# Quarters for the fifth product of all pairs, ScalarE for each block's first slot, the bias kept in DRAM

## The chip, the core and the metric

The kernel runs on one NeuronCore of a Trainium2 chip. Its engines work side by side, each through its own instruction queue in order: TensorE (PE, matmuls; its weight loads are listed as PEld), VectorE (DVE), ScalarE (ACT), GpSimd (POOL) and SyncE (SP, which issues transfers). Transfers (DMA) are issued from the queues of SP, ACT and POOL and carried out by 16 DMA engines. SBUF is the on-chip memory of 128 partitions, PSUM the small memory that PE writes to, used here in banks of 128 x 512 fp32, DRAM the memory outside.

The metric is the device time of one execution in microseconds (us), the median of several runs. Lower is better.

## What is computed

One layer of a relational graph network with a highway gate, on 1250 nodes of 1024 features, 20000 edges of 8 types, all in fp32:

```python
h = jnp.maximum(_layernorm(x, axis=-1), 0.0)
# _rgcn(h, ...):
out = h @ root + bias
for r in range(8):
    mask = (edge_type == r).astype(x.dtype)
    sums = segment_sum(h[src] * mask[:, None], dst, num_segments=n)
    cnt = segment_sum(mask, dst, num_segments=n)
    out = out + (sums / jnp.maximum(cnt, 1.0)[:, None]) @ weight[r]
u = out
z = jnp.concatenate([u, h], axis=1) @ w_gate + b_gate
x = x + jnp.tanh(u) * z + h * (1.0 - z)
```

## The kernel before

**Matrices and steps.** The kernel multiplies first and gathers afterwards. It computes y_r = h @ weight[r] for all nodes and stores y in DRAM; for every edge it later fetches row src of y_r, scales it by one over the count, and adds it to u of node dst. With root and the two halves of w_gate there are 11 matrices of 1024 x 1024: s = 0 to 7 are the relations, 8 is root, 9 the half of w_gate that meets h, 10 the half that meets u. The nodes lie in ten blocks of 128 (the last has 98 rows), taken two at a time: step (s, i) with i = 0 to 4 multiplies blocks i and i + 5 by matrix s. So matrices 0 to 9 have 50 steps, some 115 us for the five of one matrix.

**Strassen.** Each step is a Strassen product of halves (Winograd's form): seven half products instead of eight, with operands A11, A12, S4, S1, S2, S3, A22 in `h_op[i]` and the matching weight combinations in `wbuf`. One half product is four calls of 128x512 (line 511), each of which is two matmuls in the trace. Where two steps form a pair, (0,1) or (2,3), some of their half products are themselves made by Strassen's scheme over the pair, by quarters (line 255, 128x256): `Second` for A12, `Third` for S4, `First` for A11, and `Fifth` for S1. A quarter scheme replaces two half products (16 matmuls of 512 in the trace) by seven quarter products (28 of 256). It also needs sums on DVE: `sums` and `next_sums` (lines 309 to 318, four operations each, through the shared buffers `room`), copies on ACT (lines 424, 432, 439) and two adds into PSUM (lines 434, 445). Step i = 4 stands alone.

**Which pairs make S1 by quarters.** `fifths(s, i)` decides: `FIFTHS = (1, 4)`, so both pairs for s = 1 to 4, and only pair (0,1) for s = 5 to 9. While it holds for a step, `narrow[0]` is set and `sum_bank(1)` keeps one of the four `ps` banks of PSUM for good (`kept`); the first time, `touch` writes to it with one bf16 matmul (line 134). At a step where `fifths` is false the kept bank is given up.

**A pair with Fifth.** In the pair's first step, `product` runs `root.begin()`, `p1` (with `First.late`, `root.sums()`, `root.second()`), the S2 product, `root.early()`, `root.next_sums()`, and within `p7`, after the S3 product, `between(TICK)` and `root.late()`. `late` begins with the quarter product that reads what L315 and L316 made.

**The order of work beside the products.** After each part of a product, `done()` calls `between(j)`, which runs whatever is due beside it: the sums for the next product, loads of weights, and the work of the edges. The program order written this way is the order in every engine's queue. From s = 5 on the work beside is `edges`, one generator that advances by a number of ticks at each call (`spread`): 

- Group 0 (relations 0 to 4) runs beside s = 5 to 7, group 1 (relations 5 to 7) beside s = 8 and 9.
- For each block of 128 nodes sorted by degree, `K[g][d]` slots: 118 in group 0, 75 in group 1. One slot is one tick, `add_slot`: an indirect gather of 128 rows of y on POOL's queue into one of five `got` buffers (line 1560), and u = got * w + u on DVE (line 1565).
- u starts from `first_u`: in group 0 by a load of the bias, repeated over the rows, on SP's queue (line 1578); in group 1 by a gather of what group 0 stored (line 897).
- Five ticks after the last slot, `u_back` stores u of group 0 into its rows of `u_dram` (line 903, an indirect store on POOL's queue).

Before that, beside s = 4, the generator `beside_group` waits for step (4, 2), makes `passes_over`, gives five calls away and then counts edges (`counts`, lines 934 and 935), the rest of which is worked off at the end of step (4, 3).

The two lines that give `spread` its pace:

```python
said[0] += (10, 8, 13, 11, 8)[at_call[0]]
while said[1] < min(total, -(-total * said[0] // parts)):
```

Of the kernel before, what the change touches and what calls it, by code (L numbers as in the profile page):

```python
# [15 lines left out]
OP = mybir.AluOpType  # L16
# [5 lines left out]
def tile_rgcn_highway(  # L22
# [472 lines left out]
    def product(aop, w, to, between=lambda j: None, last=None, pieces=1, whole=True,  # L495
# [67 lines left out]
        def p1():  # L563
            if first is None:
                b = lead()
                add(b, A11, True)
            else:
                b = first.late() if head else first.to1
            if root and head:
                root.sums()  # L570
                first.fifth_to()
            nc.scalar.copy(c11, b)  # L572
            if root and head:
                root.second()
            done()
            filled("first")
            return b

        def p5(c=None):
# [108 lines left out]

    def fifths(s, i=0):

        return s >= FIFTHS[0] and (s <= FIFTHS[1] or i < 2)

    waiting, waiting_third, waiting_first, waiting_fifth = {}, {}, {}, {}
    at_call = [0, 0]
# [203 lines left out]
            out=to, out_offset=None, in_=of,  # L898
            in_offset=bass.IndirectOffsetOnAxis(ap=at, axis=0), compute_op=op)

    def to_rows(of, frm, at, group):
        nc.gpsimd.memset(apart, 0.0)
        ins = nc.gpsimd.indirect_dma_start(  # L903
            out=of, out_offset=bass.IndirectOffsetOnAxis(ap=at, axis=0), in_=frm, in_offset=None)
        tc.declare_no_dep(ins.ins, query=no_wait, group=group, reason="rows differ")
        tc.add_to_no_dep_group(group, ins.ins)

# [620 lines left out]
    with ExitStack() as edges_part:  # L1528
# [25 lines left out]
            nc.vector.tensor_scalar_max(rcp, rcp, 1.0)  # L1554
            nc.vector.reciprocal(rcp, rcp)

        def add_slot(u, g, d, k, at, w):
            n = nrows(d)
            t = got()
            nc.gpsimd.indirect_dma_start(  # L1560
                out=t[:n], out_offset=None, in_=y[g][:, :],
                in_offset=bass.IndirectOffsetOnAxis(ap=at[:n, d, k:k + 1], axis=0),
                bounds_check=y[g].shape[0] - 1, oob_is_err=False)
            w = w[:n, d, k:k + 1]
            nc.vector.scalar_tensor_tensor(u[:n], t[:n], w, u[:n], op0=OP.mult, op1=OP.add)  # L1565

# [6 lines left out]
        def first_u(g, d):  # L1573

            n = nrows(d)
            u = new_u(d)
            if g == 0:
                nc.sync.dma_start(u[:n], bias[None, :].to_broadcast([n, D]))
            else:
                rows_of(u[:n], u_dram[g - 1][:, :], node[:n, g, d:d + 1])  # L1580
            return u

        def edges(g, blocks, to, late=0, more={}):

            nb = len(blocks)
            starts = [late + sum(K[g][d] for d in blocks[:b]) for b in range(nb + 1)]
            leaves = [starts[b + 1] - 1 + GOT for b in range(nb)]  # L1590
            reads = [max(-1, starts[b] - (9 if d in more else 5),
                         leaves[b - UB] if b >= UB else -1) for b, d in enumerate(blocks)]
            u, then = {}, {}
            for t in range(-1, leaves[-1] + 4):
                for b, d in enumerate(blocks):
                    if starts[b] <= t < starts[b + 1]:
                        k = t - starts[b]
                        add_slot(u[d], g, d, k, idx[:, g], w_of[:, g])
                for b, d in enumerate(blocks):
                    if t == leaves[b]:  # L1600
                        then[t + 3] = to(d, u[d])
                if then.get(t):
                    then[t]()
                for b, d in enumerate(blocks):
                    if t == reads[b]:
                        u[d] = first_u(g, d)
                    if d in more and t == starts[b] - 4:
                        more[d](d, u[d])
                yield

        def u_back(g):
            def to(d, u):
                n = nrows(d)
                to_rows(u_dram[g][:, :], u[:n], node[:n, g, d:d + 1], f"u{g}")

            return to

        def spread(e, total, parts):

            said = [0, 0]  # L1620
            parts *= 10

            def between(j):
                said[0] += (10, 8, 13, 11, 8)[at_call[0]]
                while said[1] < min(total, -(-total * said[0] // parts)):
                    next(e, None)
                    said[1] += 1
                if said[0] == parts:
                    for _ in e:
                        pass  # L1630

            return between
# [50 lines left out]
        def beside_group():  # L1683

            yield
            while at_call != [2, 1]:
                yield
            passes_over()
            for _ in range(5):
                yield  # L1690
            for g in range(G):
                yield from counts(g)
# [339 lines left out]
```

## Time and profile before

| what | us |
|---|---|
| median of 3 runs (lowest, highest) | 1329.66 (1327.8, 1329.93) |
| the profiled execution, its own time | 1325.06 |
| its span, first to last instruction | 1323.3 |
| busy in the span: PE, DVE, POOL, ACT | 1309.9, 1032.2, 642.6, 277.9 |
| slot adds on DVE (line 1565), 193 | 246.8, 1.282 each |
| gathers on POOL (line 1560), 193 | 255.4, 1.324 each |

Times in all views are microseconds from the span's start. A row of the timeline gives the start, the length from the first start to the last end, and how many equal instructions it merges; ends of matmuls are modelled and overlap the next start, so the distance between starts is the real cost. The steps that matter here lie at 543.3 to 585.0 (s = 4, i = 2 and 3), 612.5 to 657.5 and 657.5 to 699.9 (s = 5, pairs (0,1) and (2,3)), 957.7 (start of s = 8), 1003.0 to 1045.4 (s = 8, pair (2,3)) and 1118.1 to 1160.5 (s = 9, pair (2,3)).

### The profile page before, as it was taken

Reading aid. Unit: us, or ns where it says so; the run is one execution under the profiler, and the core shown is the slowest. Engines: PE = TensorE matmul, PEld = TensorE weight load, DVE = VectorE, ACT = ScalarE, POOL = GpSimd, SP = SyncE. Lnnn points to the kernel's source line nnn. Section 1 sums busy time; section 2 is a strip of 40 time slices with the busy share of each in tenths; the row PEclk is TensorE's granted clock in tenths of the full one; section 3 lists DMA queues with packets and bytes.
Section 4 is the critical chain, followed back from the end, with each engine's and each line's share of the span. In section 5 each row is a group of like instructions: output and inputs, shape, how many; then the busy total and the mean of one; then the engine's idle time right before and its main releaser. Section 6 shows DMA issues by size and latency. Waiting matters only on the chain.

```text
span 1323.3 us, 14353 instructions
## 1 busy us (share of the span) xinstructions
PE 1309.9 (99%) x4280; PEld 747.0 (56%) x4280; DVE 1032.2 (78%) x2171; ACT 277.9 (21%) x509; POOL 642.6 (49%) x981
## 2 busy tenths in 40 slices
PE   9999999999999999999999999999999999999997
PEld 5444565556455546655655655665565566544443
DVE  7768977797783776558977988897788889867974
ACT  3352121121112212211221211122122112122210
POOL 0001766666666675412453545456465546624732
PEclk9999999999999999999999999999999999999999
DMA  8976566753734253444748779788789957979961
GB/s 312 300 231 165 98 115 136 153 82 82 170 113 115 57 143 65 68 161 157 250 136 309 252 272 366 268 282 283 255 282 335 362 187 256 312 269 297 331 173 60
DMA packets 119397, 273.22 MB, mean 206 GB/s; under 512 B 33438, under 2 KB 45106, under 8 KB 119184
## 3 DMA queue, kind: packets, MB, share of 16 engines
q1 hardware_dynamic: 59120, 122.06, 31.7%
q0 software_dynamic: 44064, 118.20, 28.0%
q10 hardware_dynamic: 16128, 31.98, 7.9%
q8 instruction: 34, 0.56, 0.2%
q14 instruction: 51, 0.42, 0.1%
HBM read 210.73 MB, written 76.46 MB: 217 GB/s over the span
## 4 chain that ended last, share of the span: by engine, by line
PE 87%; DMA 4%; DVE 4%; issue 3%; POOL 1%; SPq 1%; ACT 1%; POOLq 0%; DVEq 0%
PE ps_b L511 42%; PE ps L255 19%; PE ps L511 10%; PE ps_n L511 4%; PE ps_b L255 4%; PE ps_n L255 3%; PE ps_q L255 2%; PE ps_q L511 2%; DMA xt<-in_x_dram 1%; DMA got<-hr_dram,node 1%; DMA w<-in_L_gnn_weight_dram 1%; DVE h_op L492 1%; DMA h_op<-in_L_gnn_b_gate_dram 0%; POOL out_dram L903 0%; SPq L983 0%
## 5 line engine op out<-in xcount | busy, mean ns | idle before, releaser
L511 PE MATMUL ps_b<-w,h_op 128*128 128x512 f32 x1464 | 658.3, 594 | 1.0 <-ACT row L615 0.8
L511 PEld LDWEIGHTS ps_b<-w,h_op 128*128 128x128 f32 x1464 | 275.2, 190 | 301.2 <-issue 292.7
L1560 POOL DMA_INDIRECT got<-y,idx x193 | 255.4, 1324 | 277.5 <-DVE u L1565 182.1
L1565 DVE SCALAR_TENSOR_TENSOR u<-got,w_of,u 128x1024 f32<-128x1024 f32 (+1 forms) x193 | 246.8, 1282 | 38.9 <-DMA got<-y,idx 36.3
L1209 POOL DMA_INDIRECT table<-row_col,at_i x157 | 183.3, 1168 | 119.4 <-issue 84.4
L511 PE MATMUL ps<-w,h_op 128*128 128x512 f32 (+1 forms) x392 | 174.1, 586 | 0.8 <-ACT row L589 0.8
L511 PEld LDWEIGHTS ps<-w,h_op 128*128 128x128 f32 x392 | 73.5, 190 | 84.0 <-issue 78.7
L255 PE MATMUL ps<-inner 128*128 128x256 f32 x420 | 106.1, 380 | 0.0
L255 PEld LDWEIGHTS ps<-inner 128*128 128x128 f32 x420 | 79.2, 190 | 20.7 <-issue 9.4
L255 PE MATMUL ps<-w,h_op 128*128 128x256 f32 x340 | 88.2, 382 | 1.0 <-ACT w L272 1.0
L255 PEld LDWEIGHTS ps<-w,h_op 128*128 128x128 f32 x340 | 63.7, 190 | 29.3 <-issue 20.7
L537 ACT COPY row<-ps_b 128x512 f32<-128x512 f32 x53 | 31.1, 586 | 225.4 <-PE ps_b L511 225.4
L615 ACT COPY row<-ps_b 128x512 f32<-128x512 f32 x54 | 31.7, 586 | 216.0 <-PE ps_b L511 216.0
L511 PE MATMUL ps_n<-w,h_op 128*128 128x512 f32 x168 | 75.6, 593 | 0.0
L255 PE MATMUL ps<-w,w 128*128 128x256 f32 x288 | 70.6, 380 | 0.0
L255 PEld LDWEIGHTS ps<-w,w 128*128 128x128 f32 x288 | 54.4, 190 | 17.2 <-issue 11.0
L1217 POOL MEMSET apart<- 128x1 f32 x471 | 54.6, 116 | 18.1
L659 ACT COPY row<-ps_b 128x512 f32<-128x512 f32 x40 | 23.4, 586 | 186.2 <-PE ps_b L511 165.1
L543 DVE TENSOR_TENSOR row<-row 128x512 f32<-128x512 f32 x44 | 30.2, 686 | 39.6 <-ACT row L537 39.6
L1326 DVE SCALAR_TENSOR_TENSOR junk<-k_bc,key_col,before 128x128 f32<-128x128 int16 x157 | 55.0, 350 | 4.2
L511 PEld LDWEIGHTS ps_n<-w,h_op 128*128 128x128 f32 x168 | 31.7, 190 | 37.7 <-issue 37.1
L572 ACT COPY row<-ps_b 128x512 f32<-128x512 f32 x54 | 31.8, 588 | 84.8 <-PE ps_b L511 80.5
(254 smaller groups left out, 1568.1 us busy)
## 6 DMA issues: line engine op xcount, KB each, us to landing
y<-row SPq DMA_DIRECT2D x72, 512.0 KB
w<-in_L_gnn_weight_dram ACTq DMA_DIRECT2D x21, 1024.0 KB
w<-in_L_gnn_weight_dram SPq DMA_DIRECT2D x10, 1024.0 KB
w<-lefts_dram SPq DMA_DIRECT2D x16, 512.0 KB
w<-in_L_gnn_w_gate_dram ACTq DMA_DIRECT2D x6, 1024.0 KB
k_bc<-keys_dram SPq DMA_DIRECT2D x39, 128.0 KB
l_bc<-los_dram SPq DMA_DIRECT2D x39, 128.0 KB
h_dram<-h_op SPq DMA_DIRECT2D x9, 512.0 KB
```

The costliest lines, as they stand in the source:

```text
L255: nc.tensor.matmul(p, a[:, k, :], b[:, k, :], start=(fresh and k == 0), stop=(k == 1), skip_group_check=True)
L511: nc.tensor.matmul(b[:, at], aop[:, i, k, :], w.of[i][:, k, at], start=(fresh and k == 0), stop=(k == KQ - 1), skip_group_check=True)
L537: nc.scalar.copy(d, b)
L543: nc.vector.tensor_add(c22, c if lone else c22, d)
L572: nc.scalar.copy(c11, b)
L615: nc.scalar.copy(c12, b)
L659: nc.scalar.copy(c21, b)
L1209: ins = nc.gpsimd.indirect_dma_start(out=table[:, :], out_offset=bass.IndirectOffsetOnAxis(ap=at_i[:n, c:c + 1], axis=0), in_=row_col[:n, ...
L1217: nc.gpsimd.memset(apart, 0.0)
L1326: nc.vector.scalar_tensor_tensor(junk, o["k_bc"][:, i, :], key_col[:, c:c + 1], before, op0=OP.is_equal, op1=OP.mult, accum_out=rank[:, c: ...
L1560: nc.gpsimd.indirect_dma_start(out=t[:n], out_offset=None, in_=y[g][:, :], in_offset=bass.IndirectOffsetOnAxis(ap=at[:n, d, k:k + 1], axis=0),
L1565: nc.vector.scalar_tensor_tensor(u[:n], t[:n], w, u[:n], op0=OP.mult, op1=OP.add)
```

## The change

- `fifths` becomes true for all s > 0: pair (2,3) of s = 5 to 9 makes S1 by quarters too, and the kept bank stays from s = 1 on.
- `spread` no longer counts the additional call `TICK`, except at i = 0, so that i = 2 keeps its pace.
- In the second step of a pair (`root and inner and not head`) the fills that belong to p1 run ahead of `done()` instead of after it.
- In group 0 each block's first slot makes u on ScalarE: the gather is issued two ticks ahead of the copy (`slot_of`), the copy scales it into a new u (`scaled_slot`). Group 0's ticks fall from 123 to 113.
- The bias no longer starts u. Instead `beside_group` writes it into all rows of `u_dram`, from DRAM to DRAM on SP's queue, in ten calls where it gave five away, and `u_back` stores with an add.

```diff
@@ product, p1
-            done()
-            filled("first")
+            if root and inner and not head:
+                filled("first")
+                done()
+            else:
+                done()
+                filled("first")
             return b
@@
     def fifths(s, i=0):
-        return s >= FIFTHS[0] and (s <= FIFTHS[1] or i < 2)
+        return s > 0
@@
-    def to_rows(of, frm, at, group):
+    def to_rows(of, frm, at, group, op=OP.bypass):
         nc.gpsimd.memset(apart, 0.0)
         ins = nc.gpsimd.indirect_dma_start(
-            out=of, out_offset=bass.IndirectOffsetOnAxis(ap=at, axis=0), in_=frm, in_offset=None)
+            out=of, out_offset=bass.IndirectOffsetOnAxis(ap=at, axis=0), in_=frm, in_offset=None,
+            compute_op=op)
@@
-            if g == 0:
-                nc.sync.dma_start(u[:n], bias[None, :].to_broadcast([n, D]))
-            else:
-                rows_of(u[:n], u_dram[g - 1][:, :], node[:n, g, d:d + 1])
+            rows_of(u[:n], u_dram[g - 1][:, :], node[:n, g, d:d + 1])
             return u
+        def scaled_slot(t, g, d):
+            n = nrows(d)
+            u = new_u(d)
+            nc.scalar.mul(u[:n], t[:n], w_of[:n, g, d, 0:1])
+            return u
@@ edges
-            starts = [late + sum(K[g][d] for d in blocks[:b]) for b in range(nb + 1)]
+            by_act = int(g == 0)
+            starts = [late + sum(K[g][d] - by_act for d in blocks[:b]) for b in range(nb + 1)]
...
-                        k = t - starts[b]
+                        k = t - starts[b] + by_act
                         add_slot(u[d], g, d, k, idx[:, g], w_of[:, g])
...
-                    if t == reads[b]:
+                    if by_act:
+                        if t == starts[b] - 3:
+                            ahead[d] = slot_of(g, d, 0, idx[:, g])
+                        if t == starts[b] - 1:
+                            u[d] = scaled_slot(ahead.pop(d), g, d)
+                    elif t == reads[b]:
                         u[d] = first_u(g, d)
@@ u_back
-                to_rows(u_dram[g][:, :], u[:n], node[:n, g, d:d + 1], f"u{g}")
+                to_rows(u_dram[g][:, :], u[:n], node[:n, g, d:d + 1], f"u{g}", OP.add)
@@ spread
-                said[0] += (10, 8, 13, 11, 8)[at_call[0]]
+                if j != TICK or at_call[0] == 0:
+                    said[0] += (10, 8, 13, 11, 8)[at_call[0]]
@@ beside_group
-            for _ in range(5):
+            for d in range(ND):
+                nc.sync.dma_start(u_dram[0][block(d), :],
+                                  bias[None, :].to_broadcast([nrows(d), D]))
                 yield
@@
-        s, i = beside(first_group, sum(K[0]) + LATE + 1, s, i, R0[2] - 1)
+        s, i = beside(first_group, sum(K[0]) - ND + LATE + 1, s, i, R0[2] - 1)
```

`slot_of` is the gather of `add_slot`, taken out into a function of its own; `add_slot` now calls it.

More of the change, by code (lines that the diff above doesn't have):

```diff
@@ L1555, in as_reciprocals, with slot_of @@
             nc.vector.reciprocal(rcp, rcp)
-        def add_slot(u, g, d, k, at, w):
+        def slot_of(g, d, k, at):
             n = nrows(d)
@@ L1563, in add_slot @@
                 bounds_check=y[g].shape[0] - 1, oob_is_err=False)
+            return t
+        def add_slot(u, g, d, k, at, w):
+            n = nrows(d)
+            t = slot_of(g, d, k, at)
             w = w[:n, d, k:k + 1]
@@ L1576, in first_u @@
             u = new_u(d)
-            if g == 0:
-                nc.sync.dma_start(u[:n], bias[None, :].to_broadcast([n, D]))
-            else:
-                rows_of(u[:n], u_dram[g - 1][:, :], node[:n, g, d:d + 1])
+            rows_of(u[:n], u_dram[g - 1][:, :], node[:n, g, d:d + 1])
+            return u
+        def scaled_slot(t, g, d):
+            n = nrows(d)
+            u = new_u(d)
+            nc.scalar.mul(u[:n], t[:n], w_of[:n, g, d, 0:1])
             return u
@@ L1592, in edges @@
                          leaves[b - UB] if b >= UB else -1) for b, d in enumerate(blocks)]
-            u, then = {}, {}
+            u, then, ahead = {}, {}, {}
             for t in range(-1, leaves[-1] + 4):
```

## The prediction

> **What bounds the kernel now.** I read the page first: engine rows, clock slices, chain.
>
> ```profile
> span 1323.3 us, 14353 instructions
> PE 1309.9 (99%) x4280; PEld 747.0 (56%) x4280; DVE 1032.2 (78%) x2171; ACT 277.9 (21%) x509; POOL 642.6 (49%) x981
> PEclk9999999999999999999999999999999999999999
> PE 87%; DMA 4%; DVE 4%; issue 3%; POOL 1%; SPq 1%; ACT 1%; POOLq 0%; DVEq 0%
> ```
>
> TensorE (PE) has work for 99% of the span at the full granted clock, and is 87% of the chain that ended last. A busy PE is not yet a PE without waits, so next I read the timeline of PE by start times: the distance from one start to the next is what a group really costs.
>
> ```profile
> 654.01 3.60 PE L511 MATMUL ps_b<-w,h_op 128*128 128x512 f32 x8
> 657.45 3.60 PE L511 MATMUL ps_n<-w,h_op 128*128 128x512 f32 x8
> 660.88 1.03 PE L255 MATMUL ps<-inner 128*128 128x256 f32 x4
> 661.75 1.03 PE L255 MATMUL ps_b<-w,inner 128*128 128x256 f32 x4
> ...
> 682.60 3.60 PE L511 MATMUL ps<-w,h_op 128*128 128x512 f32 x8
> 686.04 3.60 PE L511 MATMUL ps_b<-w,h_op 128*128 128x512 f32 x8
> ...
> 741.36 0.38 PE L134 MATMUL ps<-ident 128*128 128x512 bf16 x1
> 741.58 1.03 PE L255 MATMUL ps<-inner 128*128 128x256 f32 x4
> ```
>
> Eight 512-wide matmuls take 3.43 us from start to start (657.45 to 660.88), 0.429 each; four 256-wide ones 0.86, 0.2155 each. Neighbouring groups start at these distances throughout matrices 4 to 9; nothing waits there beyond 0.1 us now and then. So in this stretch the time is the count of matmuls, and any PE work removed is time removed, unless a wait appears. Whether one can appear is read from VectorE (DVE), by stages.
>
> ```profile
> 543.30:585.00 41.70, 41.70 (x147) 27.13 (x146) 23.03 (x57) 9.77 (x20) 14.13 (x15) 1.00 0.35 101
> 657.45:699.87 42.42, 42.42 (x133) 24.83 (x132) 34.55 (x42) 8.57 (x17) 24.14 (x20) 1.00 0.52 168
> 1003.00:1045.40 42.40, 42.40 (x133) 24.82 (x132) 32.04 (x38) 8.57 (x17) 27.48 (x22) 1.00 0.97 343
> 1118.10:1160.50 42.40, 42.40 (x133) 24.83 (x132) 34.61 (x44) 8.57 (x17) 27.65 (x21) 1.00 0.94 317
> 612.50:657.50 45.00, 45.00 (x162) 30.18 (x161) 44.16 (x89) 9.82 (x21) 19.54 (x15) 1.00 0.76 249
> ```
>
> Columns: stretch, length, busy PE, weight loads, DVE, ACT, POOL, clock, DMA share, GB/s. Rows one to four are steps i=2 and 3 of matrices 4, 5, 8 and 9; the last is i=0 and 1 of matrix 5. Matrix 4 already makes this pair's S1 product by quarters, matrix 5 does not: that comparison is the heart of the forecast.
>
> **The change, part by part.** (1) *Quarters.* With `fifths` true for all s > 0, pair (2,3) of matrices 5 to 9, five pairs, replaces two S1 products (16 matmuls of 512 in the trace, 16 x 0.429 = 6.87 us) by seven quarter products (28 of 256, 28 x 0.2155 = 6.03): -0.83 us. The rows confirm it: 42.42 at matrix 5 against 41.70 at matrix 4, where one stray transpose (L1657, 551.17 to 551.28, 0.11) is included: 42.42 - 41.59 = 0.83. Five pairs: -4.15 us.
>
> [...]
>
> (2) *The kept bank.* It is now never given up between matrices 5 and 9, so four `touch` matmuls (i=0 of matrices 6 to 9) go: 741.36 to 741.58, 0.22 each, -0.88 us. The price: three rotating banks instead of four in i=2 to 4. Matrices 1 to 4 run that way, and the bank row that was closest at matrix 4 (L283, ended 569.91, reused 574.59) left 4.7 us. Zero.
>
> Sum of what is removed from PE: -5.03 us.
>
> (3) *What quarters add elsewhere.* Per pair DVE gets four 128x256 operations (0.417), four 128x512 (0.683) and two into PSUM (0.425): 5.25 us. ACT gets 0.36 + 0.37 + 0.57, in handshakes with PE that are already in the 41.59. DVE in the pair goes from 34.55 to 39.8 of 41.6 us at matrix 5, from 32.04 to 37.3 at matrix 8, from 34.61 to 39.9 (96%) at matrix 9, before the relief of (4). It still fits; the last row shows 98% busy without a PE wait. What counts is one deadline: the sums L315 and L316 must end before PE's `late`. Their margin under load, at i=0 of matrix 5:
>
> ```profile
> 622.41 2.28 DVE L207 TENSOR_TENSOR w<-w,w 128x2048 f32<-128x2048 f32 x1
> 624.61 0.42 DVE L434 TENSOR_TENSOR ps_n<-ps,inner 128x256 f32<-128x256 f32 x1
> 625.27 0.68 DVE L316 TENSOR_TENSOR inner<-w 128x512 f32<-128x512 f32 x1
> 626.37 1.03 PE L255 MATMUL ps<-inner 128*128 128x256 f32 x4
> ```
>
> L316 ends at 625.95, PE starts at 626.37: 0.42 us left, the tightest of the five; with an idle DVE (matrix 4, i=2) it was 556.44 - 554.63 = 1.8. At i=2 two slot adds (1.28 each, 1.2 apart) stand just before L434. From the end of `First.late` PE needs 0.86 + 3.43 + 1.72 = 6.0 us to L434's input (546.87 to 553.00 without a stray transpose); DVE needs 2.2 (sums) + 0.35 (L398) + three slot adds 3.6 = 6.15. L434 would be 0.15 late of a margin of 1.8. Below, 0; above, two adds more (2.4) would cost 0.8 per pair. The sum is nearer to 0; I take 0.1, five times: +0.5.
>
> (4) *First slot on ACT.* Ten slot adds leave DVE (-12.8 us over matrices 5 to 7) and ten scaled copies of 128x1024 come to ACT. Not in the trace of before; nearest rows are L1899 (1.05 us, no pointer operand) and L1028 (1.24, two): 1.05 to 1.24; I take 1.15, 11.5 us on an engine that is 21% busy. In the order of the changed program each stands between copies of two consecutive products; the next copy waits for a product that ends at least 3.4 us after the one before: hidden behind PE, 0. Were that cover gone, the copies and PSUM banks queued behind it would be late, up to 1.2 us each, 12 in all. It also waits for its gather; that is issued two slots earlier than its use and lands after 6.1 us (median of L1560), with five buffers of some 2.9 us each (115 us over 39 slots) ahead. The block's second slot on DVE now waits for ACT, so DVE loses some run-ahead, which (3) already assumes away. With 113 instead of 123 adds spread over the same calls, matrices 5 to 7 come out even on DVE: +15.75 - 12.8 = +2.9 us of 345.
>
> (5) *Bias.* Ten SP loads of 512 KB into u go from matrices 5 to 7; ten DRAM to DRAM stores of that size come on SP's queue at matrix 4, i=2 and 3. Seven stand behind the y store that SP issued at 544.11, and DMA is 0.08 busy from 550 to 560 and 0.20 from 560 to 570: room. Behind them waits y's store of 565.93. Two more stand before the weight load of 570.80: 1 MB, 5 us at the 211 GB/s of 570 to 580, written and read 10. What waits for that load is L195, 21 us later at 592.06, and there it waited for PE. Zero; without that cover up to 10 us of DVE. The counts of edges (L934, L935) move five calls back in the order, so some five pairs of 0.75 us fall at about 585, into the 5.44 us that DVE idles before 592.06. Zero.
>
> (6) *u stores that add.* Accumulating stores to DRAM are not in the trace. Bounds: a plain u store lands in 6.3 us and costs POOL 1.03; an accumulating gather (h_op<-z_dram) lands in 12.1 and costs 1.56. Nearest by kind is the second: +5.8 us of landing, +0.5 on POOL, ten times. POOL is idle half the time, mostly waiting for DVE to free a buffer; gathers queued behind the store are late, next DVE's adds:
>
> ```profile
> POOL got L1560 <- DVE u L1565: 182.1, 78, 6.8
> DVE u L1565 <- DMA got<-y,idx: 36.3, 21, 4.0
> ```
>
> Buffers limit the gathers far oftener than gathers limit DVE, so this is spent from run-ahead. One place is different: the first read of u by the second group waits for all stores. The last starts at 955.63, the first read at 963.64, and the first add at 972.70; 5.8 us later the sums L310, ready at 977.17 for a PE need at 981.90 (margin 4.7), would be about 1 us late. Bound 0 to 2 us; the read already waits until 963.64 for y's store, so I take 0.3.
>
> (7) *Order in i=1 and 3*: slots come after the fills instead of before; DVE's bank releases run earlier, the slots a little later. Zero either way within (3)'s bound.
>
> Sum: -5.03 + 0.5 + 0.3 = -4.2 us. The profiled execution took 1325.06 us (span 1323.3): it becomes 1320.8. The runs shown have a median of 1329.66, 0.35% above it; the same difference gives 1325.4, stated as 1325.5.
>
> **The rivals.** All start from 1329.66 - 5.03 = 1324.6. *Half eaten* (within 0.2%, that is 2.66 us, about what this measurement can tell from no change): each pair meets the upper bound of (3), 0.8 x 5 = 4.0: 1328.6. For it: the 0.42 us at 626. Against: i=0 carries the same sequence in a fuller DVE without a wait.
>
> *Late gathers in front of L434* (slower): DMA is 0.97 busy in i=2 and 3 of matrix 8, 0.94 at matrix 9. If a slot add ahead of L434 waits for its gather, L434, L315 and L316 wait with it, and PE stops at `late`. The longest such wait was 4.0 us; less 1.8 of margin, 2.2 x 5 = 11: 1335.6. It decides from 7.7 us in all (5.03 + 2.66), 1.5 a pair. Against: gathers were waited for in i=2 where DVE had run ahead of PE; now the sums hold it back there, and gathers get time to land.
>
> *It does not do what it says*: in the new places a 256-wide matmul costs 0.245 us (6.87 / 28) and the pairs gain nothing; the touches stay: 1329.66 - 0.88 = 1328.8, within 0.2%. Against: 0.2155 in every row, those of matrix 4's same pair too.
>
> **Chances.** Forecast 0.66, half eaten 0.15, no gain 0.04, late gathers 0.15. So faster by over 0.2% 0.66, within 0.2% 0.19, slower 0.15. The forecast's own range is 1322.5 (no new wait, less the 2.1 us by which the shown runs differ) to 1327.0 (the bounds of (3) or (6) half met). The 8 in 10 range goes up to 1331.5, into the late gathers at 1.4 us a pair, and leaves out more of them.
>
> **What would show it.** Right: (1) steps i=2, 3 of matrices 5 to 9 take 41.6 to 41.8 us by PE starts; (2) one `touch` less at i=0 of 6 to 9; (3) L316 at i=2 ends before `late`; (4) ACT's copies after each scaled slot start within 0.1 us of PE's product; (6) first read of u before 970. Wrong: PE gaps over 0.3 us before L255 at `late`, or DVE idle on gathers just before L434.

## The result, and the profile after

The changed kernel takes 1342.72 us (median of 4 runs, 1339.54 to 1344.44) beside 1329.8 for the kernel before on the same chip: a ratio of 1.0097, 95% interval 1.008 to 1.0113. It is slower by 13 us; the prediction was 1325.5, and its range ended at 1331.5. The profiled execution took 1339.54 us.

The page of the changed kernel: span, engine rows, the granted clock in 40 slices, the chain that ended last, and two groups of part 5 (busy us, mean ns, idle before with its releasers).

```profile
span 1337.7 us, 14550 instructions
PE 1309.6 (98%) x4336; PEld 758.7 (57%) x4336; DVE 1042.4 (78%) x2211; ACT 294.8 (22%) x534; POOL 651.3 (49%) x981
PEclk9999999999999999999999999999999899999999
PE 69%; DVE 11%; issue 9%; DMA 6%; POOL 3%; SPq 1%; ACT 1%; another core or an unknown queue 1%; POOLq 0%; DVEq 0%
...
L511 PE MATMUL ps<-w,h_op 128*128 128x512 f32 (+1 forms) x352 | 158.7, 593 | 7.9 <-DVE row L352 6.8
```

PE's busy time is almost unchanged, although 5 us of matmuls went. PE is 69% of the chain where it was 87%: VectorE stands in it with 11% and DMA with 6%, and one slice shows a lower clock. The last line has the first new wait: PE's whole-bank products of p5 (the product of S1) idle 6.8 us for L352, the addition on VectorE that reads a PSUM bank empty. In the kernel before, that group of instructions had no such wait.

Step lengths, from one PE start to the next step's first PE start, show where the 14.4 us of span came from (us; the columns e2 to b3 are experiments, told of below):

| step | before | changed | e5 | e2 | e6 | e7 | e8 | b3 |
|---|---|---|---|---|---|---|---|---|
| matrix 4, i=1 | 24.11 | 25.68 | 24.11 | 24.11 | 24.11 | 24.11 | 24.11 | 24.11 |
| matrix 4, i=2 | 23.54 | 28.61 | 23.54 | 23.54 | 23.54 | 23.54 | 23.54 | 23.55 |
| matrix 6, pair (2,3) | 42.42 | 41.58 | 41.58 | 41.58 | 41.58 | 41.58 | 41.58 | 42.96 |
| matrix 7, pair (2,3) | 42.42 | 41.58 | 41.58 | 41.58 | 41.58 | 41.58 | 41.58 | 46.19 |
| matrix 7, i=4 | 27.49 | 28.65 | 28.24 | 28.88 | 28.01 | 27.49 | 28.07 | 27.49 |
| matrix 8, i=1 | 24.11 | 24.11 | 24.11 | 24.11 | 24.46 | 24.11 | 27.91 | 24.11 |
| matrix 8, pair (2,3) | 42.42 | 42.26 | 42.51 | 42.42 | 43.00 | 42.50 | 43.00 | 44.23 |
| matrix 8, i=4 | 27.49 | 34.65 | 34.55 | 27.49 | 27.49 | 27.85 | 27.49 | 31.25 |
| matrix 9, i=0 | 21.11 | 20.86 | 20.86 | 21.11 | 20.86 | 24.92 | 24.12 | 20.86 |
| matrix 9, pair (2,3) | 42.42 | 43.58 | 43.09 | 42.42 | 42.64 | 42.83 | 44.23 | 46.39 |
| matrix 9, i=4 | 30.12 | 31.69 | 31.70 | 30.12 | 30.12 | 30.13 | 30.12 | 30.12 |

Two things happened. Matrix 4, where the change adds only the bias stores and the new order of fill and slot, lost 6.6 us. Matrix 8 lost 6.7 us and matrix 9 up to step i=3 0.9 (and 1.9 in what follows), where the prediction had them gain; matrices 5 and 6 gained 0.95 and 0.99, about as forecast, and matrix 7 kept nothing.

**Matrices 8 and 9.** VectorE in the changed kernel, end of matrix 8's pair and start of i=4 (timeline; start, duration, operation, and in brackets the idle time before it with its releaser):

```profile
1036.97 1.29 DVE L1575 SCALAR_TENSOR_TENSOR u<-got,w_of,u 128x1024 f32<-128x1024 f32 x1 [2.84 <-DMA got<-y,idx]
...
1048.38 1.31 DVE L1575 SCALAR_TENSOR_TENSOR u<-got,w_of,u 98x1024 f32<-98x1024 f32 x1 [1.17 <-DMA got<-y,idx]
...
1052.44 1.28 DVE L1575 SCALAR_TENSOR_TENSOR u<-got,w_of,u 98x1024 f32<-98x1024 f32 x1
1055.24 1.28 DVE L1575 SCALAR_TENSOR_TENSOR u<-got,w_of,u 128x1024 f32<-128x1024 f32 x1 [1.52 <-issue]
1056.44 0.41 DVE L286 TENSOR_TENSOR row<-row,ps 128x256 f32<-128x256 f32 x1
1056.77 0.68 DVE L351 TENSOR_TENSOR row<-row,ps_n 128x512 f32<-128x512 f32 x1
1057.37 0.68 DVE L352 TENSOR_TENSOR row<-row,ps 128x512 f32<-128x512 f32 x1
```

PE at the same place:

```profile
1046.42 7.03 PE L511 MATMUL ps_b<-w,h_op 128*128 128x512 f32 x16
1058.10 4.64 PE L511 MATMUL ps<-w,h_op 128*128 128x512 f32 x5 [4.65 <-DVE row L352]
```

L352's input was in PSUM by 1046.6 (from 1046.42 to 1053.45 PE writes `ps_b` alone), but on VectorE it stands behind slot adds that wait for their gathers, and ends at 1058.05, 8.2 us after the step's start at 1049.86. PE's p5 wants its bank at 1053.3. In the kernel before (matrix 8, then matrix 9; their steps i=4 start at 1045.41 and 1160.54) L352 was no early release either, but p5 began without a wait:

```profile
1047.90 0.68 DVE L352 TENSOR_TENSOR row<-row,ps 128x512 f32<-128x512 f32 x1
1048.84 3.60 PE L511 MATMUL ps<-w,h_op 128*128 128x512 f32 x8
...
1165.06 0.68 DVE L352 TENSOR_TENSOR row<-row,ps 128x512 f32<-128x512 f32 x1
1163.98 3.60 PE L511 MATMUL ps<-w,h_op 128*128 128x512 f32 x8
```

At matrix 8 it ended 0.26 us before p5 began, 3.2 us after the step's start, so it now comes 5.0 us later in the step; at matrix 9 it ended 1.8 us after p5 began. Why PE now needs that one bank stands in the program:

```python
# p5
c = inner.hold() if inner and inner.holds else \
    sum_bank(odd) if narrow[0] else held("ps_n")
...
# the call of product
head=i % 2 == 0, lone=i == NP - 1, odd=int(i % 2 or i == NP - 1), root=root,
```

Step i=4 has no `inner`, and its `odd` is 1. With `fifths` true there, p5 is given `sum_bank(1)`, the kept bank. In that same bank the pair (2,3) has made its sum for S1, and L352 is the addition that reads it last. In the kernel before, `fifths` was false at i=4, and p5 took the next bank of the rotation.

The pair (2,3) of matrices 5, 8 and 9 in the changed kernel, as stretches (length, busy PE, loads, VectorE, ScalarE, GpSimd, clock, DMA share, GB/s):

```profile
664.21:705.79 41.58, 41.58 (x146) 27.11 (x144) 35.10 (x49) 10.93 (x21) 20.37 (x17) 1.00 0.36 117
1007.60:1049.86 42.26, 41.77 (x146) 27.11 (x144) 35.11 (x48) 9.77 (x20) 24.35 (x20) 1.00 0.92 317
1129.48:1173.06 43.58, 42.04 (x146) 27.03 (x144) 38.52 (x53) 9.78 (x20) 27.86 (x21) 1.00 0.92 304
```

Matrix 5 has the forecast 41.58 us. VectorE's busy time in matrix 8 is the same 35.1 us and still PE waits: the average share of VectorE does not tell of the wait, the gathers between its operations do (DMA 0.36 busy there, 0.92 here).

**Matrix 4.** ScalarE's copies:

```profile
526.87 0.37 ACT L267 COPY w<-ps 128x256 f32<-128x256 f32 x1 [2.02 <-PE ps L255]
531.14 0.59 ACT L619 COPY row<-ps_b 128x512 f32<-128x512 f32 x1 [3.90 <-PE ps_q L255]
...
561.82 0.59 ACT L537 COPY row<-ps_b 128x512 f32<-128x512 f32 x1 [7.41 <-remote]
562.57 0.57 ACT L439 COPY ps<-ps 128x512 f32<-128x512 f32 x1 [0.17 <-remote]
```

L267 and L619 start 2.2 us after the products that they wait for (ended 524.66 and 528.95), and each waits for PE's semaphore alone. The semaphore records of the trace tell what was late: the updates by PE stand at 526.84 and 531.12, and ScalarE starts 0.03 and 0.02 us after them. In the profile of e5, the same kernel without a gap here, they stand at 524.86 and 529.16, 0.01 us after the products. So ScalarE does not pause by itself; PE's signal comes late. The same holds for L537: its product ended at 558.29, the update stands at 561.80, and it starts at 561.82. It also has to wait for y's store out of the row buffer that it writes, but that store (issued at 539.93) had landed at 545.11, and this wait was over at 554.06. VectorE's releases follow late, y's stores are issued up to 6 us late, and the burst of bias stores (L1711, seven issued from 546.17) comes right behind them. In the stretch where L537 is late DMA is full:

```profile
550.00:560.00 10.00, 10.00 (x33) 5.56 (x31) 3.00 (x9) 0.96 (x2) 7.56 (x9) 1.00 1.01 213
560.00:570.00 10.00, 6.83 (x21) 5.08 (x21) 2.90 (x6) 2.41 (x5) 2.51 (x4) 0.83 0.61 137
```

In e5's profile DMA is as full there, 1.00 and 0.97 busy in the same two stretches, and PE loses nothing.

### The profile page after: what moved, and what is told of

Same layout as the page of the kernel before. It is cut to its first block, busy times and chain, and to the rows that moved or that the text cites. A ratio compares the mean times of both kernels' runs of the same rounds, so it can differ in the third digit from the quotient of the medians.

```text
span 1337.7 us, 14550 instructions
## 1 busy us (share of the span) xinstructions
PE 1309.6 (98%) x4336; PEld 758.7 (57%) x4336; DVE 1042.4 (78%) x2211; ACT 294.8 (22%) x534; POOL 651.3 (49%) x981
## 4 chain that ended last, share of the span: by engine, by line
PE 69%; DVE 11%; issue 9%; DMA 6%; POOL 3%; SPq 1%; ACT 1%; another core or an unknown queue 1%; POOLq 0%; DVEq 0%
PE ps_b L511 32%; PE ps L255 15%; PE ps L511 9%; DVE u L1575 4%; DMA got<-y,idx 3%; PE ps_b L255 3%; PE ps_n L511 3%; PE ps_n L255 3%; PE ps_q L511 2%; PE ps_q L255 1%; POOL got L1565 1%; DMA xt<-in_x_dram 1%; DMA w<-in_L_gnn_weight_dram 1%; DMA w<-in_L_gnn_b_gate_dram 1%
## 5 line engine op out<-in xcount | busy, mean ns | idle before, releaser
L1575 DVE SCALAR_TENSOR_TENSOR u<-got,w_of,u 128x1024 f32<-128x1024 f32 (+1 forms) x183 | 233.9, 1281 | 30.0 <-DMA got<-y,idx 22.7
L1214 POOL DMA_INDIRECT table<-row_col,at_i x157 | 180.1, 1147 | 119.2 <-issue 86.5
L511 PE MATMUL ps<-w,h_op 128*128 128x512 f32 (+1 forms) x352 | 158.7, 593 | 7.9 <-DVE row L352 6.8
L255 PE MATMUL ps<-inner 128*128 128x256 f32 x480 | 120.8, 380 | 0.6 <-DVE inner L316 0.6
L511 PEld LDWEIGHTS ps<-w,h_op 128*128 128x128 f32 x352 | 66.5, 192 | 86.1 <-issue 70.8
L255 PEld LDWEIGHTS ps<-inner 128*128 128x128 f32 x480 | 90.6, 190 | 25.7 <-issue 10.8
L255 PE MATMUL ps<-w,h_op 128*128 128x256 f32 x360 | 94.3, 385 | 3.7 <-issue 1.8
L255 PEld LDWEIGHTS ps<-w,h_op 128*128 128x128 f32 x360 | 67.5, 191 | 35.9 <-issue 24.3
L619 ACT COPY row<-ps_b 128x512 f32<-128x512 f32 x54 | 31.6, 586 | 231.0 <-PE ps_b L511 223.6
L537 ACT COPY row<-ps_b 128x512 f32<-128x512 f32 x53 | 31.1, 586 | 225.3 <-PE ps_b L511 201.4
L511 PE MATMUL ps_n<-w,h_op 128*128 128x512 f32 x128 | 57.6, 593 | 0.0
```

The costliest lines, as they stand in the source:

```text
L255: nc.tensor.matmul(p, a[:, k, :], b[:, k, :], start=(fresh and k == 0), stop=(k == 1), skip_group_check=True)
L511: nc.tensor.matmul(b[:, at], aop[:, i, k, :], w.of[i][:, k, at], start=(fresh and k == 0), stop=(k == KQ - 1), skip_group_check=True)
L537: nc.scalar.copy(d, b)
L619: nc.scalar.copy(c12, b)
L1214: ins = nc.gpsimd.indirect_dma_start(out=table[:, :], out_offset=bass.IndirectOffsetOnAxis(ap=at_i[:n, c:c + 1], axis=0), in_=row_col[:n, ...
```

## The experiments

The five sets of experiments fell on five chips. The kernel before, run beside them, took 1325.4 to 1325.9 us with e1 to e8 and with b and c, and 1328.3 with e9 to e12. So ratios to it are compared, and step lengths, not microseconds between sets.

**e1: bias stores in matrix 3.**

```diff
+                if s == 3 and j in (2, 4):        # in on(j)
+                    d = 2 * i + j // 4
+                    nc.sync.dma_start(u_dram[0][block(d), :], ...)
...
-            for d in range(ND):
-                nc.sync.dma_start(u_dram[0][block(d), :], ...)
+            for _ in range(5):
                 yield
```

> The changed kernel, but its ten bias stores are issued two per step in matrix 3, and the counts of edges start five calls later as in the kernel before. Theory A: in matrix 4 the burst of DRAM to DRAM stores shares the DMA engines with y's store, whose landing frees the row that ACT's copy L537 of step i=2 waits for; the gap of 3.34 us at 559.64 and the slow clock after it go. Step i=2 goes from 28.6 back to 23.5 us, time 1342.7 - 5.1 = 1337.6; 1336.0 if the 1.57 us of step i=1 go as well. Rival B: the gap comes from the new order of fill and slot or from late instructions, not from these stores: i=2 stays at 28 us and the time at 1342.7. Rival C: matrix 3 now has the stall (its y stores meet the same stores): 1342 with steps of matrix 3 longer.

1332.94 us, 1.006 of before (1.0047 to 1.0073). Step i=2 of matrix 4 took 23.54 us, i=1 24.11, and matrix 3 was as before. It looked like theory A, until e2 and e5, which have the stores in their new place, showed the same 23.54.

**e2: quarters only up to matrix 7. e3: this and e1.**

```diff
-        return s > 0
+        return s > 0 and (s <= 7 or i < 2)
```

> The changed kernel with the S1 product of pair (2,3) whole again in matrices 8 and 9, quarters in matrices 1 to 7. Theory: the quarters' sums make VectorE late in these two, bank releases L352, L353 and L283 come late and PE stops. Without them the stalls of matrix 8 (0.65 + 4.81 + some 1.7 of slow clock) and of matrix 9 (0.76 + 1.11 + 1.46) go, 10.5 us; the quarters' gain of 2 x 0.84 and one touch of 0.25 are lost: 1342.7 - 10.5 + 1.9 = 1334.1. Rival: the gathers are late for another reason (accumulating u stores, the scaled slot on ScalarE, the calls' new places): the stalls stay, 1342.7 + 1.9 = 1344.6.

> Both edits of the two runs above together. If the two stalls are independent, the gains add: 1342.7 - 5.1 - 8.6 = 1329.0, or 1327.4 with step i=1 of matrix 4. If one theory is wrong, its part stays: 1334 to 1337.6.

e2: 1323.71 us, 0.9985 of before (0.9976 to 0.9994); e3: 1323.49, 0.9983 (0.9974 to 0.9991). All gaps of matrices 8 and 9 are gone, and the kernel is faster than before. The time is lower than the 1334 expected because matrix 4 has no gap here (6.6 us) and the kernel before is 4 us faster on this chip. The edit takes away the quarters and, from i=2 on, the kept bank, so it does not tell the two apart. Three pairs by quarters (3 x 0.84) and four touches of 0.25 less one would be worth 3.3 us; 2.1 are measured, since matrix 7 still waits 1.3 us at i=4.

**e4: quarters, the new order and the pace of `spread` alone**, all else as before the change (the first slot on VectorE, the bias loaded into u, plain stores of u).

> The kernel before with the quarters in all pairs and the changed order of fill and slot alone: the first slots stay on VectorE, the bias is loaded into u as before, u's stores don't add. Theory: the quarters' sums alone overload VectorE in matrices 7 to 9, here with ten slot adds more on it in matrices 5 to 7: the 5.0 us of TensorE are gained, the 11.6 us of stalls in matrices 7 to 9 are lost: 1329.8 - 5.0 + 11.6 = 1336.4. Rival: the other two parts of the change make those stalls: 1329.8 - 5.0 = 1324.8. Matrix 4 has no bias stores here: its step i=2 takes 23.5 us by theory A, 28.6 if the new order makes the gap.

1333.75 us, 1.0058 (1.0045 to 1.0071). It has the gaps of matrices 7 to 9 nearly as in the changed kernel (1.5, 1.1, 4.5, 0.7, 0.8 and 1.5 us). So the quarters, with the bank that they keep, make them; the parts that were to relieve VectorE in matrices 5 to 7 change nothing in 8 and 9.

**e5: the changed kernel again.**

> The changed kernel itself, run beside the kernel before on the chip that ran the four experiments. The second of them kept the bias stores where the change put them and its profile has no gap in matrix 4. Theory: the gap there started with ScalarE's copies L267 and L619, which began 2 us late without a wait that the program shows, and comes with the chip or the execution, not with the change: step i=2 of matrix 4 takes 23.5 us here, and the time is that of the run with the bias stores in matrix 3, 1.0055 of before. Rival: it is the change's: 28.6 us again, 1.0097 of before.

1332.6 us, 1.0058 (1.0044 to 1.0072), on yet another chip than e1 to e4. No gap in matrix 4, the gaps of matrices 7 to 9 as in the first profile. So some 7 us of the 13 belong to the quarters wherever the kernel ran, equal to e4's within the interval, and the rest to what happened in matrix 4 on the first chip.

**e6: half of the second group's gathers left out** (a slot with an odd number is added from the rows that the slot before it gathered, so the edges of these slots are missing from u).

```diff
-            t = slot_of(g, d, k, at)
+            if g == G - 1 and k % 2 and from_slot[0] is not None:
+                t = from_slot[0]
+            else:
+                t = slot_of(g, d, k, at)
+            from_slot[0] = t if g == G - 1 and k % 2 == 0 else None
...
```

> The changed kernel, but in the second group every slot with an odd number is added from the row block that the even slot before it gathered; half of that group's gathers are left out, VectorE's adds are all there. Theory: what PE waits for in matrices 8 and 9 is VectorE, which stands at slot adds whose gathers land late; the sums of the quarters only took away the slack. With half the gathers the waits of 0.5 to 2.9 us before L1575 go and so do the PE gaps of 4.7, 1.5, 1.2 and 0.7 us: before - 5.0 + 1 (matrix 7), 0.997 of before. Rival: VectorE's own work is too long for the pair: the gap at i=4 of matrix 8 stays above 2.5 us, 1.002 to 1.005 of before.

1320.51 us, 0.9961 (0.9946 to 0.9976), a little under the expected 0.997. VectorE's L352 and PE's p5 at i=4 of matrix 8:

```profile
1045.70 0.68 DVE L352 TENSOR_TENSOR row<-row,ps 128x512 f32<-128x512 f32 x1
...
1047.33 3.60 PE L511 MATMUL ps<-w,h_op 128*128 128x512 f32 x8
```

With every add in place but without waiting for gathers, L352 ends 1 us before p5. What is left are two gaps of 1.3 and 1.0 us in front of PE's `late` in i=2, behind L316: the deadline that the prediction's step (3) had named.

**e7: the kept bank given back at i=4**, so that four banks rotate there and p5 takes the next of them.

```diff
-        narrow[0] = fifths(s, i)
+        narrow[0] = fifths(s, i) and not (s > 6 and i == NP - 1)
```

> The changed kernel, but the kept bank is given back in step i=4 of matrices 7 to 9, as before the change, so four banks rotate there; one touch of 0.22 us more per matrix. Theory of the banks: PE's wait at p5 of i=4 is for the bank that L352 frees; with a fourth bank p5 takes one that was free earlier and the gaps of 4.7 (matrix 8), 1.5 (matrix 9) and 0.8 (matrix 7) go, those in i=2 and 3 (0.7, 0.7, 1.2) stay: 1.0055 - 0.0052 + 0.0005 = 1.001 of before. Rival: VectorE is too late for any number of banks, PE waits one product later for the same reason: above 1.004.

1326.7 us, 1.0008 (0.9998 to 1.0018), as expected, 0.5% below the changed kernel (5.9 us by the medians). The same two instructions:

```profile
1050.54 0.68 DVE L352 TENSOR_TENSOR row<-row,ps 128x512 f32<-128x512 f32 x1
...
1046.27 3.60 PE L511 MATMUL ps<-w,h_op 128*128 128x512 f32 x8
```

L352 is as late as in the changed kernel, but PE starts p5 4.3 us before it, in another bank. This and e6 show that the long gap needs both: VectorE late behind gathers, and p5 in the bank that L352 frees. Part of the wait comes back one step later, with VectorE full (9.96 of the 10 us up to 1087) and no gather waited for:

```profile
1086.93 1.59 PE L255 MATMUL ps<-inner 128*128 128x256 f32 x4 [1.87 <-DVE inner L316]
```

There i=0 of matrix 9 takes 24.92 us, 3.8 more than before.

**e8: the second group's slots spread by weights 12, 9, 9, 9, 11** over the five steps, in place of 10, 8, 13, 11, 8.

> The changed kernel, but the second group's slots are spread over the steps with weights 12, 9, 9, 9, 11 instead of 10, 8, 13, 11, 8: some four to five fewer of them stand in the pair (2,3) that has the quarters' sums (5.25 us). Theory: PE's gaps in i=3 and in i=4's start come from VectorE's backlog at the end of the pair; they shrink to under 1 us each, and the time is at most that of the kernel without quarters in 8 and 9: 0.998 of before. Rival: VectorE and DMA are full over the whole of matrices 8 and 9, the gaps move to i=4, 0 and 1: above 1.003.

1334.36 us, 1.0066 (1.0051 to 1.0081): a miss, the rival's case. The pair's bank releases are in time (i=4 of matrix 8 is 27.49), but PE now waits in front of products that need VectorE's sums, mostly in i=0 to i=2:

```profile
L255 PE MATMUL ps<-inner 128*128 128x256 f32 x480 | 121.2, 381 | 9.7 <-DVE inner L316 6.5 <-DVE inner L310 3.2
```

**e9 to e12: other ways to make room.** e9 makes u on ScalarE in the second group too; the read of the first group's u then adds to it.

```diff
...
+                    at = reads[b] if g else starts[b] - 1
+                    if t == at - 2:
+                        ahead[d] = slot_of(g, d, 0, idx[:, g])
+                    if t == at:
+                        u[d] = scaled_slot(ahead.pop(d), g, d)
+                        if g:
...
+                            rows_of(u[d][:n], u_dram[g - 1][:, :], node[:n, g, d:d + 1], OP.add)
...
```

e10 is e9 with e7's edit, e11 e9 with e2's, e12 e2 with e7's.

> The changed kernel, and in the second group too each block's first slot makes u on ScalarE; the read of the first group's u then adds to it (ten accumulating gathers in place of ten plain ones). VectorE loses ten slot adds, 12.8 us, in matrices 8 and 9, where the quarters' sums brought 10.5; bytes on DMA stay. Theory: VectorE's backlog behind the sums is the cause, gathers are late because it frees their buffers late; with the relief the gaps of 4.9 us (matrix 8, i=4) and 1.5 (matrix 9, i=4) fall under 1 us each: 1325.4 - 5.0 + 2 = 1322.4, 0.998 of before or less. Rival: DMA at 0.97 of its time lands the gathers late whoever adds them: the gap at i=4 of matrix 8 stays above 2.5 us, 1.003 or more.

> The run with the second group's first slots on ScalarE, with the kept bank given back in i=4 of matrices 7 to 9 besides. Theory: what is left at i=4 goes, for three touches of 0.22: 1321.5, 0.997 of before. Rival: as in the run with four banks alone, the wait moves to i=0 of matrix 9 (4.06 us there) and the gain is less than 0.5 us over the run without the fourth bank.

> The second group's first slots on ScalarE, quarters in matrices 1 to 7 only. If VectorE had no backlog there without the quarters, the relief is worth nothing: 0.9985 of before, like the run with quarters to 7 alone. If accumulating reads of u delay the second group, slower than that by up to 2 us: 1.000.

> Quarters in matrices 1 to 7 and the fourth bank in i=4 of matrix 7, where the run with quarters to 7 kept a gap of 1.3 us before p5. Theory: the wait for the bank that L352 frees goes, for a touch of 0.25: 0.9985 - 0.0008 = 0.9977 of before. Rival: the wait moves to i=0 of matrix 8, as it moved to matrix 9 in the run with four banks: 0.9985 to 0.999.

e9: 1370.68 us, 1.0322 (1.0309 to 1.0336); e10 1.0333, e11 1.0339. All three missed by more than 3%, with quarters in matrices 8 and 9 or without, so they tell nothing of VectorE's share; they show what this edit itself costs. Three instructions of e9 in the order in which they wait for each other:

```profile
976.10 1.15 ACT L1594 ACTIVATE u<-got,w_of 128x1024 f32<-128x1024 f32 x1 [10.70 <-DMA got<-y,idx]
977.52 1.56 POOL L901 DMA_INDIRECT u<-u_dram,node  x1 [4.86 <-ACT u L1594]
987.10 1.28 DVE L1575 SCALAR_TENSOR_TENSOR u<-got,w_of,u 128x1024 f32<-128x1024 f32 x1 [5.12 <-DMA got<-y,idx]
```

ScalarE stands 10.7 us for one gather with PE's copies queued behind it, GpSimd stands for ScalarE with all later gathers behind it, and VectorE then for those. That is the loss of cover that the prediction had priced in (4) for the first group. There four of the ten copies waited for their gather, 5.5 us in all in the first profile, and PE did not stop for it.

e12: 1328.58 us, 1.0003 (0.999 to 1.0015) in place of 0.9977. Its matrix 7 has almost no gap left (27.71 us at i=4), as expected, but matrix 4 had gaps again (27.98 and 24.44 us in i=1 and i=2, together 4.8 more than before), as had e9 to e11 beside it (25.1 to 25.8 and 24.3 to 29.6). The same two copies of ScalarE start late as in the first profile; e12's:

```profile
527.20 0.37 ACT L267 COPY w<-ps 128x256 f32<-128x256 f32 x1 [1.99 <-remote]
531.50 0.58 ACT L619 COPY row<-ps_b 128x512 f32<-128x512 f32 x1 [3.93 <-PE ps_n L255]
```

Here too it is PE's update that is late: 527.18 and 531.48, for products that ended at 525.28 and 528.71.

**b1 to b4, c1 and c2: the gaps in matrix 4.** b1 and c1 are the kernel before, b2 the changed kernel, c2 is e1's kernel. b3 undoes the new order of fill and slot, b4 puts e1, e2 and the fourth bank of matrix 7 together.

```diff
-            if root and inner and not head:
-                filled("first")
-                done()
-            else:
-                done()
-                filled("first")
+            done()
+            filled("first")
```

> The kernel before, for its profile on this chip. Theory: the pause of some 2 us that ScalarE's copies L267 and L615 show at 525 to 531 belongs to the chip, so the kernel before has it too, step i=1 of matrix 4 is 24.8 to 28 us, but without bias stores y's stores land in time and i=2 stays at 23.5 to 24.4. Rival: the change makes the pause: 24.11 and 23.54 here while the changed kernel has gaps. If no profile of this set has a gap, nothing follows.

> The changed kernel on the same chip. Where ScalarE pauses at 525 to 531, theory: 25 to 28 us in i=1, up to 28.6 in i=2, 1.0097 of before; without the pause 1.0058.

> The changed kernel with the old order of fill and slot in i=1 and 3 (the slot's call ahead of the fill). If that order makes the pause in matrix 4, i=1 and i=2 are at 24.11 and 23.54 here and not in the changed kernel beside it; if it has nothing to do with it, they are as there. In matrices 7 to 9 the bank releases stand behind one slot more: the gaps of matrix 8 grow by 1 to 2 us if it matters, 1.007 to 1.010 of before.

> Quarters in matrices 1 to 7, the bias stores in matrix 3, the fourth bank at i=4 of matrix 7: everything that helped, together. Theory: i=2 of matrix 4 stays at 23.5 to 24.4 with or without the pause, matrices 5 to 7 have no gap: 0.9977 of before. Rival: the gap in matrix 4 needs no bias stores: 1.000 as in the run with quarters to 7 and four banks, where the pause occurs.

> The kernel before once more, for a profile on another chip. If its median is 1328 us or more and the profile shows ScalarE's copies L267 and L615 2 us after their products, the pause belongs to the chip and the kernel before has it too: step i=1 of matrix 4 takes 24.8 us or more, i=2 at most 24.4. If the time is high without a pause, the pause is not what makes these chips slower. At 1325 to 1326 without a pause nothing follows.

> The changed kernel with the bias stores in matrix 3, on the same chip. Where the pause occurs, theory: y's stores find DMA free, i=2 of matrix 4 takes at most 24.4 us in place of 28 and the time is 1.006 of before, not 1.0097. Rival: the pause alone is enough for the long gap: 28 us and 1.0097. Without a pause 1.006 and nothing new.

No profile of these two sets has the gaps in matrix 4 (24.11 us at i=1 in all six), so nothing follows for them. Measured were: b1 1.0001 (0.9992 to 1.001), c1 1.0002 (0.9992 to 1.0011); b2 1.0062 (1.0047 to 1.0078); c2 1.0053 (1.0036 to 1.007); b4 0.9989 (0.998 to 0.9998), in place of the 0.9977 expected: better than before by about as much as e2 and e3 and not better than they.

b3 did tell something: 1.0086 (1.0071 to 1.0101) beside b2's 1.0062, all its runs above all of b2's. One group of PE's products in b3, then in b2:

```profile
L255 PE MATMUL ps<-w,h_op 128*128 128x256 f32 x360 | 94.1, 384 | 9.4 <-DVE row L283 8.5 <-ACT w L272 1.0
```

```profile
L255 PE MATMUL ps<-w,h_op 128*128 128x256 f32 x360 | 93.5, 382 | 2.0 <-ACT w L272 1.0 <-DVE row L283 1.0
```

With the slot's call ahead of the fill, the bank that L283 frees in i=3 is 8.5 us late in sum, where the new order leaves 1.0.

## Why the prediction was wrong, by its steps

- **(1) Quarters**: right. The pair takes 41.58 us in matrices 5, 6 and 7 (42.42 before).
- **(2) The touches**: right; i=0 of matrices 6 to 9 takes 20.86 us in place of 21.11 to 21.14. **The kept bank's price, "Zero"**: this is the step that failed. It was priced as a rotation with one bank less, by the margin of one release (L283, 4.7 us) at matrix 4, where VectorE has no slot adds and waits for no gather. That p5 of i=4 is made in the kept bank itself, and so waits for L352, was not in the sum. The trace of before had the price: 0.26 us of margin at matrix 8, and 1.8 us too late at matrix 9, before any sum of the quarters was added. In the changed kernel L352 stands behind six slot adds at matrix 8. The steps i=4 of matrices 7 to 9 lost 0.75, 7.06 and 1.58 us in e5, 9.4 in all; giving the bank back there (e7) took the ratio from 1.0058 to 1.0008, some 6 us, since part of the wait came back elsewhere. The long gap alone cost 7.16 us in the first profile, 4.8 of waiting and 2.3 of slow clock after it.
- **(3) What the quarters add on VectorE**: the ten operations a pair were right (38 to 48 in matrix 8), but the only deadline looked at (L316 before `late`) was the smaller one. It was missed once, at matrix 9's i=2, which lost 0.85 us in e5 where the forecast had 0.5 for all five pairs; the wait there grows to 1.2 us in e6, and in e7, at i=0, to 1.9 us. The sums hold up the slot adds, and thereby the releases behind them: L352 comes 5.0 us later in its step at matrix 8, for 5.25 us of sums. The rotation of three banks has its own, smaller price in i=3, where PE waits for L283's bank: 0.9 and 0.7 us in e5.
- **(4) First slot on ScalarE**: right. Ten at 1.15 us, and e5's ratio equals that of e4, which is without it. It also brought no relief where it was wanted: the ten adds leave matrices 5 to 7, the gaps are in 8 and 9.
- **(5) The bias stores, "Zero"**: right in e2 and e3, which differ by 0.2 us with the stores in matrix 4 or 3, though not by the room that was read for them: they fill DMA (1.00 and 0.97 busy from 550 to 570 in e5, 0.08 and 0.20 before), and PE lost nothing by it. In the first set and that of e9 to e12 matrix 4 had gaps. In the first profile L537 did not wait for y's store, and that the bias stores have a part in the gaps is not shown.
- **(6) Adding stores of u**: nothing where 0.3 was taken; i=0 of matrix 8 takes 20.86 us.
- **(7) The order, "Zero either way"**: wrong by some 3 us in the change's favour (b3 against b2). Without it the change would have lost more.

The account closes for e5, whose span is 6.8 us above that of the kernel before in b1 and c1 (1330.6 against 1323.8). PE's matmuls are 5.0 us shorter; the waits in matrices 7 to 9, with the slow clock behind them, are 9.4 (i=4), 1.6 (i=3) and 0.85 us (matrix 9, i=2), 11.8 in all.

*Late gathers* was the rival nearest to what happened: gathers waited for in front of something that PE needs. It had the wrong victim, L434 in place of the bank releases L352 and L283, and so its 1335.6 was some 2 us short of the 1337.4 to 1337.9 that 1.0058 to 1.0062 make of 1329.66. Its argument against, that gathers get time to land while the sums hold VectorE back, failed: a VectorE held back frees the gathers' five buffers late. In the first profile the gathers issued at 1042.06 and 1046.17 had waited 1.45 and 2.59 us for VectorE, and DMA is 0.92 busy in that pair.

**Open** is what made PE's signals late in matrix 4 (6.6 us in the first profile). It occurred in two of the six sets of runs, in all five profiles taken there with the change, and in these five alone the records of semaphore updates are incomplete: 708 by PE where 748 matmuls make one, in the first. In the other fifteen none is missing. In the same two sets the kernel before was slower too, 1329.8 and 1328.3 us, which points away from the change; but its first profile shows no late signal and was 2.7 us below the next of the runs shown with it. So neither the change nor the chip is shown to be the cause, and that the recording has a part in it is not excluded.

## What to carry to other kernels

A buffer that is kept for one purpose is free for its next user only after the last instruction that reads it: in the changed kernel p5 of matrix 8 began at 1058.10, and L352 had ended at 1058.05. So ask of a kept bank who else is given it, follow it to that last reader, and count what stands ahead of that reader in its queue, transfers that it waits for included. Do so in the stage where the reader's engine is most behind: a margin read in a quiet stage (4.7 us at matrix 4) says nothing of a loaded one (0.26 us at matrix 8, none at matrix 9). And where a gain repeats over stages, keep it where it is free: quarters up to matrix 7 give 0.9985 of before, two more pairs turn this into 1.0058.

## What the runs showed of the hardware

The gap at matrix 8 cost PE more than its length. After the wait of 4.65 us, whole-bank matmuls started 0.85 us apart in place of 0.429 for some five of them, and the clock granted in that stretch was 0.84 and then 0.82:

```profile
1049.00:1059.00 10.00, 5.35 (x12) 2.21 (x11) 7.83 (x11) 1.17 (x2) 4.61 (x5) 0.84 1.03 396
1059.00:1069.00 10.00, 10.00 (x20) 4.27 (x19) 8.44 (x9) 0.59 (x1) 7.56 (x4) 0.82 1.03 413
```

The trace's clock records, cut at the times where they change, show what lies behind these means:

```profile
1052.43:1055.84 3.41, 1.02 (x3) 0.19 (x1) 1.89 (x3) 1.17 (x2) 1.95 (x2) 1.00 1.03 410
1055.84:1062.67 6.83, 4.57 (x6) 1.99 (x7) 5.88 (x8) 0.00 (x0) 3.12 (x3) 0.50 1.02 405
1062.67:1066.08 3.41, 3.41 (x10) 1.50 (x9) 2.76 (x2) 0.00 (x0) 3.10 (x2) 1.00 1.03 420
```

In the traces of the kernel before and of the changed kernel the granted clock is 1.0 or 0.5 and nothing else. In that of the changed kernel the stretches up to its last change are 559.79, 3.41, 488.11, 6.83 and 269.65 us long, 164, 1, 143, 2 and 79 times 3.413 us. It is at half for 3.41 us from 564.33, for 6.83 us from 1055.84, and again from 1332.32, after PE's last matmul; the kernel before is at half from 1317.75 alone, at its end.

In the 3.41 us ahead of the first of these stretches PE was busy for 1.13 us, ahead of the second for 1.02 (above). Two stops of the same trace were followed by full clock: PE was busy for 2.22 of the 3.41 us from 530.19 and for 2.11 of those from 1175.31. In e7 the wait of 1.87 us at 1086.93 (shown above) had slow matmuls behind it: the first two groups of 256-wide products took 1.38 us for four and 1.71 for four, from start to start, in place of 0.86, and the mean clock from 1077 to 1103 was 0.93. So some of these gaps cost their length alone, and the longest cost 2.3 us on top of 4.8. Where the limit lies, these cases do not show.
